# A GRU on one core: the last batches of a two-level fast product paired anew, and two pairs of PSUM seeds moved behind a projection

## The chip, the cores and the metric

The kernel runs on one core of a Trainium2 chip. The metric is the time of one execution on the device in microseconds (us). Three runs of the kernel before took 1289.52, 1290.0 and 1290.32 us, so the median is 1290.0 us. One further execution was taken with the hardware profiler on.

The engines are called PE (TensorE, matmuls; PEld is its weight load), DVE (VectorE), ACT (ScalarE), POOL (GpSimd) and SP (SyncE, which issues most transfers). PSUM is the memory that PE writes its sums to; a tile of PSUM here is one bank.

## What is computed

The reference is a gated recurrent layer with a residual: for 128 steps, on a batch of 64 rows of width 512, all in 32-bit floats.

```python
def step(h, inp):                       # 128 times
    x_t, prop = inp
    comb = concatenate([x_t, h])
    z = sigmoid(comb @ Wz + bz)
    r = sigmoid(comb @ Wr + br)
    h_cand = tanh(concatenate([x_t, r * h]) @ Wh + bh)
    h_new = (1.0 - z) * h + z * h_cand
    h_next = where(prop, tanh(h_new @ Wp + bp), h_new)   # prop: t % 4 == 3, not at t = 127
    return h_next, h_new
return x + ys                           # ys: the h_new of all steps
```

The part of each gate that comes from x doesn't depend on the recurrence. The part that comes from h does, and sets an order: R and Z need h, the candidate H needs r * h, the next step needs h_new. In every fourth step the projection P follows.

## The kernel before, in words

**Recurrent part.** The batch of 64 is cut into two halves of 32 rows, half 0 and half 1, which run through the same steps with an offset. `half(h)` (L781) is a generator that writes the instructions of one half; the loop at L882 alternates between the two by columns of matmul issued, with half 1 starting 700 columns behind. A gate of one half is four products (L218); each product is two matmuls (L207 to L216), and the profile shows a product as four records on line L209. The gates R, Z, H and, at a projection step, P are written in this order.

Each half has its own PSUM tile, rec_0 or rec_1, whose first part takes R and whose second part takes H and P. Z of both halves has a third tile, rec_z. Before a gate's products run, ACT copies the part that comes from x into the gate's place (`seed`, L376, copy on L379); the products add to it. The seed of R for step t+1 is normally written right after R of step t has been read (L801), the seed of H after tanh of H has been read (L854), the seed of Z after half 1's h (L856). Two steps are exceptions. R's seeds for step 4 are written in step 3, after Z's sigmoid of half 1 (L818 to L820). R's seeds for step 124 are written in step 123, after the Z seed of half 1 (L857 to L859), which is ahead of the projection's products. At a projection step, the bias of P is copied into H's place (L852) and the seed of H for the next step follows the tanh of P (L871).

After a gate, ACT applies the sigmoid or tanh (L235), DVE multiplies and subtracts (L798, L812, L840, L849) and transposes (L238) for the next gate.

**Part from x.** It is computed in groups of four steps (g is the group, LAST = 31 the one of steps 124 to 127), by a two-level scheme that saves products. A group needs up to seven outer products, numbered 1 to 7 (8 to 11 are forms used at both ends). `batch(n, ms)` (L454) takes one or two of them and makes seven kinds of inner unit, in the order 2, 7, 1, 5, 4, 6, 3. A batch has as many units of each kind as it has outer products (product 10 counts twice, for it has two terms), each of 192 columns. The sums lie in the scratch banks a, x or y (alternating between batches), q and r. They are evicted by ACT and DVE at the ends of kinds:

- after kind 7, ACT copies x to cx (L485);
- after kind 1, ACT copies q to cq (L485);
- after kind 5, DVE adds r to cx and a to cq (L502, L503);
- after kind 6, ACT copies q again and DVE adds it (L508);
- after kind 3, DVE adds r and x to the last copy (L511, L512).

Units of a later kind or batch that write the same bank wait for these. R's sigmoid also writes into a free part of the bank r. POOL then combines outer products into the tiles cp that the seeds read (L544, L549; 128 x 768 elements). A cp tile holds two steps. In the last group, steps 126 and 127 are computed plainly (`plain`, units of 256 columns, a DVE add on L417 per gate), and steps 124 and 125 by `pair_left` and `pair_right` (L583, L587), two POOL operations each.

**Order.** All units form one queue (`put`, L391). Each step takes units from it at three places: between the gates Z and H, after H, and, at a projection step, after P. How many is written down per step: `PLACES` for the eight steps that repeat, `HEAD` for steps 0 to 4, `TAIL` for steps 118 to 127 (T is 128). The queue is filled by `begin` (L649), and for the last group at step 118 (T - 10). `behind_step` (L704) issues the POOL operations behind each step, in the end the sum of x and h (L756), and the transfers of the output on SP (L766).

The engines run their instructions in the order written, each when its operands are ready.

Of the kernel before, what the change touches and what calls it, by code (L numbers as in the profile page):

```python
# [18 lines left out]
def kernel(  # L19
# [15 lines left out]
    B, T, D = x.shape  # L35
    H = h0.shape[1]
    P = 128
    S = 2
# [8 lines left out]
    LAST = T // Q4 - 1  # L47
    R, Z, H_ = range(3)
# [115 lines left out]
    def gate_ps(i, h):  # L164
        return rec[2][:, 0] if i == Z else rec[h][:, 0 if i == R else 1]
# [210 lines left out]
    def seed(i, t, h):  # L376
        if t < T:
            rows = slice(None) if i == Z else ts(h, 2 * V)
            nc.scalar.copy(  # L379
                gate_ps(i, h)[rows].rearrange("p d (c n) -> p d c n", c=C),  # L380
                G[t][rows, :, :, i, :].rearrange("p c d n -> p d c n"),
            )
# [8 lines left out]
    def put(units):  # L391
        for unit, cols, bank, end, read in units:
            queue.append((unit, cols, reader.get(bank, -1), end))
            for b in read:
                reader[b] = len(queue) - 1
# [38 lines left out]
    def plain(t, gates=(R, Z, H_)):  # L434
        order = [(e, k) for e in gates for k in range(K)]
        if t == Q4 - 1:
            order = [(e, k) for k in range(K) for e in gates]
        return [
            plain_unit(
                t, e, k, k == 0, *((lambda: add_bias(t, gates), gates) if (e, k) == order[-1] else ())  # L440
            )
            for e, k in order
        ]
# [88 lines left out]
    def batches(g):  # L532
        if g * Q4 >= T:
            return []
        ms = [(g, i) for i in (1, 2, 6, 5, 7, 3, 4)]
        if g + 1 < LAST:
            ms += [(g + 1, i) for i in (1, 6, 2, 5, 3, 7, 4)]
        return sum((batch((g, n), ms[2 * n : 2 * n + 2]) for n in range(7) if 2 * n < len(ms)), [])

    def flat(v):  # L540
# [17 lines left out]
    def outer_1(g):  # L558
        with_bias(g, 1, bias0)
# [17 lines left out]
    def outer_c22(g):  # L577
        add(c_block(g, 1, 1), m_(g, 7), m_(g, 5))

    def outer_c21(g):  # L580
        add(c_block(g, 1, 0), m_(g, 7), m_(g, 4))

    def pair_left(a, p1, p2, g=1):  # L583
        with_bias(g, p2, bias0)
        add(c_block(g, a, 0), m_(g, p1), m_(g, p2))

    def pair_right(a, p1, x_, g=1):  # L587
        with_bias(g, x_, bias_x[:, 1])
        add(c_block(g, a, 1), m_(g, p1), m_(g, x_))
# [4 lines left out]
    )  # L594
    HEAD = {0: (12, 12, 0), 1: (8, 6, 0), 2: (16, 12, 0), 3: (8, 6, 8), 4: (6, 8, 0)}
    TAIL = {
        T - 10: (1, 7, 0), T - 9: (3, 7, 5), T - 8: (1, 7, 0), T - 7: (1, 6, 0), T - 6: (0, 6, 0),
        T - 5: (0, 4, 3), T - 4: (0, 5, 0), T - 3: (0, 5, 0), T - 2: (0, 5, 0), T - 1: (0, 0, 0),
    }

    idle(40)
# [47 lines left out]
    def begin(t):  # L649
        u = (t - 3) % 8  # L650
        even = FIRST + 2 * ((t - 3) // 8)
        if t == 0:
            put(plain(2) + plain(3))
        elif t == 1:
            put(batch((1, 0), [(1, 1), (1, 2)]))
        elif t == 2:
            put(batch((1, 1), [(1, 10), (1, 11)]) + batch((1, 2), [(1, 8), (1, 9)]))
        elif t == 3:
            put(batches(FIRST))
        elif u == 7:  # L660
            put(batches(even + 2))
        if t == T - 10:
            put(
                batch((LAST, 0), [(LAST, 1), (LAST, 2)])
                + batch((LAST, 1), [(LAST, 10)])
                + plain(T - 1, (R,))[:2]
                + plain(T - 2)
                + plain(T - 1, (R,))[2:]
                + plain(T - 1, (H_,))
                + plain(T - 1, (Z,))  # L670
            )
# [32 lines left out]
    def behind_step(t, duo, u, h_new):  # L704
        g, j = divmod(t, Q4)
        even, odd = FIRST + 2 * duo, FIRST + 2 * duo + 1
        if t == T - 8:
            pair_left(0, 1, 2, LAST)
        elif t == T - 6:
            pair_right(0, 1, 10, LAST)  # L710
        if t == 3:
            pair_left(1, 8, 9)
            pair_right(1, 8, 11)

        if duo >= 0:
            if u == 0 and duo >= 1 and odd - 2 < LAST:
                outer_c22(odd - 2)
                outer_c21(odd - 2)
            if even * Q4 < T:
                if u == 0:  # L720
                    sum_s34(even)
                elif u == 1:
                    outer_1(even)
                    outer_c11(even)
                    sum_raw12(odd)
                elif u == 2:
                    outer_u1(even)
                    outer_5(even)
                    sum_raw4(even)
                elif u == 3:  # L730
                    outer_c12(even)
                    outer_u2(even)
                    outer_c22(even)
                    if odd < LAST:
                        sum_s12(odd)
                elif u == 4:
                    if odd < LAST:
                        sum_s34(odd)
                    outer_c21(even)
                    if odd < LAST:  # L740
                        outer_1(odd)
                elif u == 5 and odd < LAST:
                    sum_raw4(odd)
                elif u == 6 and odd < LAST:
                    outer_u1(odd)
                    outer_c11(odd)
                elif u == 7 and odd < LAST:
                    outer_5(odd)
                    outer_c12(odd)
        if duo >= -1 and (even + 2) * Q4 < T:  # L750
            if t == 2 or (u == 6 and duo >= 0):
                sum_raw12(even + 2)
            if u == 7:
                sum_s12(even + 2)
        if t < T - 1:
            nc.gpsimd.tensor_add(xr[g][:, j], xr[g][:, j], h_new)  # L756

        n = 0
        if t >= T - CHUNK:
            n = 3 if t == T - 2 else 0  # L760
        elif j == Q4 - 1:
            n = 4
        if n:
            for h in range(S):
                for q in range(NQ):
                    nc.sync.dma_start(  # L766
                        out=out[ts(h, V), t - n + 1 : t + 1, ts(q, J)],
                        in_=xr[g][part(q), j - n + 1 : j + 1, h, :],
                    )
        if j == 1 and g >= 1 and (g + 1) * Q4 < T:  # L770
            new_xr(g + 1)
            load_x(xr[g + 1], (g + 1) * Q4, Q4)
        if t in (1, 2):
            load_xs(t + 2)
        if duo >= 0:
            if u == 3:
                load_xs(odd + 2)
            elif u == 6:
                load_xs(even + 4)

    def half(h):  # L781

        for t in range(T):
# [5 lines left out]
            if h == 0:  # L789
                begin(t)  # L790
# [18 lines left out]
            if h == 1:  # L809
                for i in range(S):  # L810
                    crossed(z[:, i, :], i, Z, AF.Sigmoid)
                nc.vector.scalar_tensor_tensor(  # L812
                    out=keep, in0=z, scalar=1.0, in1=h_old, op0=ALU.subtract, op1=ALU.mult
                )
                join(t, duo, u, 1)
                if t == 1:
                    sum_raw34(1)
                if t == 3:  # L818
                    for i in range(S):
                        seed(R, t + 1, i)  # L820
                if last:
                    nc.gpsimd.tensor_sub(xr[g][:, j], xr[g][:, j], keep)
                if t == 0:
                    sum_outer()
                    join_x(1, 0)
                    join_x(1, 1)
                    sum_raw12(1)
                    sum_inner(6, nc.gpsimd)
                    sum_inner_1(6, nc.gpsimd)
                if t == 2:  # L830
                    for n in range(2, 4):
                        join_x(2, n)
# [21 lines left out]
                seed(H_, t + 1, h)  # L854
            if h == 1 and t != T - 2:
                seed(Z, t + 1, 0)  # L856
            if h == 1 and t == T - 5:  # L857
                for i in range(S):
                    seed(R, t + 1, i)  # L859
            state[t + 1] = h_new, hT  # L860
            yield from fill(places[1], h)
            if h == 1 and t == T - 2:
# [1 line left out]
            if prop:  # L864
                yield from gate(P_, h, hT, wp)
                h_next = new_two("hprop", t)
                hT = new_turned("hT", "hpT", t)
                crossed(h_next[:, h, :], h, P_, AF.Tanh)
                turn(hT[:, h, :], h_next[:, h, :])
                if t < T - 2:  # L870
                    seed(H_, t + 1, h)  # L871
                state[t + 1] = h_next, hT
                yield from fill(places[2], h)
            if h == 1:
# [7 lines left out]
    while any(live):  # L882
        h = 0 if live[0] and (not live[1] or at[0] <= at[1]) else 1
# [46 lines left out]
```

## Time and profile before

| | us |
|---|---|
| median of three runs | 1290.0 |
| the profiled execution | 1288.07 |
| its span | 1286.2 |
| busy time of PE within it | 1253.8 |
| busy time of POOL | 886.1 |
| busy time of ACT | 835.5 |
| busy time of DVE | 781.3 |
| transfers, mean | 47 GB/s |

The span runs from the first to the last instruction that the profile shows. The rest of the profiled execution's time, 1.87 us, lies around it. A row of the timeline gives the start in us from the beginning of the span, the duration, the engine, the line, the operation, what it writes and reads, the size, and how many instructions of this form follow each other. In brackets stands the idle time of the engine ahead of it, and what ended that idle time. A busy PE isn't PE at its peak, because matmuls overlap: several records are in flight at a time, and the duration of one is longer than the time to the next.

### The profile page before, as it was taken

To read this page: it belongs to the slowest core of one execution; us is meant where nothing else is said; L and a number is where in the kernel's file an instruction comes from. 1 tells how busy PE (TensorE), PEld (TensorE's weight loads), DVE (VectorE), ACT (ScalarE), POOL (GpSimd) and SP (SyncE) were. 2 spreads that over 40 slices of the span, in tenths; PEclk is the share of its full clock that TensorE was granted. 3 is DMA by queue.
4 is the path that set the end of the run, shared out by engine and by line. 5 is a ranking of instruction groups with operands and counts; after the bars stand their busy time and mean duration, and the time that the engine had idled before them with its cause. 6 is when DMAs were issued, how large, how long until landed. Compare 5 with 4: busy or idle time off the path is not lost.

```text
span 1286.2 us, 60724 instructions
## 1 busy us (share of the span) xinstructions
PE 1253.8 (97%) x25968; PEld 1167.4 (91%) x25968; DVE 781.3 (61%) x2166; ACT 835.5 (65%) x2688; POOL 886.1 (69%) x1027
## 2 busy tenths in 40 slices
PE   6989999999999999999999999999999999999988
PEld 2679999999999999999999999999999999999766
DVE  4646666656665666666666666666656666666544
ACT  1446666666666666666766667666676666666655
POOL 5449777777677776777787677776777787677430
PEclk9989999999999999999999999999999999999999
DMA  8302211111121111111111121111112112111100
GB/s 224 82 19 52 52 36 41 47 36 52 40 61 39 29 45 51 52 36 53 38 34 52 46 58 36 33 45 45 52 36 57 38 28 52 52 35 36 26 25 21
DMA packets 113365, 60.82 MB, mean 47 GB/s; under 512 B 12969, under 2 KB 109481, under 8 KB 113097
## 3 DMA queue, kind: packets, MB, share of 16 engines
q1 hardware_dynamic: 110628, 53.46, 16.1%
q8 instruction: 205, 3.36, 1.1%
q10 hardware_dynamic: 2212, 3.34, 1.0%
q14 instruction: 64, 0.52, 0.1%
q0 software_dynamic: 256, 0.14, 0.1%
HBM read 40.11 MB, written 16.78 MB: 44 GB/s over the span
## 4 chain that ended last, share of the span: by engine, by line
PE 93%; DMA 2%; POOL 1%; issue 1%; ACT 1%; DVE 1%; SPq 0%; ACTq 0%; POOLq 0%; DVEq 0%
PE rec L209 42%; PE rec_z L209 15%; PE scratch_r L209 13%; PE scratch_q L209 10%; PE scratch_a L209 5%; PE scratch_x L209 4%; PE scratch_y L209 4%; DMA wx<-in_L_cond_Wh_dram 1%; DMA wh<-in_L_cond_Wh_dram 1%; DMA wh<-in_L_cond_Wr_dram 0%; POOL cp L544 0%; DMA wx<-in_L_cond_Wr_dram 0%; ACT rec_z L235 0%; POOL mb L549 0%; DVE rec_z L840 0%
## 5 line engine op out<-in xcount | busy, mean ns | idle before, releaser
L209 PE MATMUL rec<-wh,rhT 128*32 128x256 f32 x4096 | 377.1, 381 | 4.5 <-ACT rec L379 4.5
L209 PE MATMUL rec<-wh,hT 128*32 128x256 f32 x3072 | 281.3, 379 | 0.3 <-DVE hT L238 0.3
L209 PE MATMUL rec_z<-wh,hT 128*32 128x256 f32 x3072 | 281.3, 379 | 0.1
L209 PEld LDWEIGHTS rec<-wh,rhT 128*32 128x32 f32 x4096 | 251.2, 110 | 23.6 <-ACT rec L379 4.9
L379 ACT COPY rec<-cp 64x256 f32<-64x256 f32 x512 | 189.8, 371 | 42.6 <-DVE cp L417 17.0
L235 ACT ACTIVATE scratch_r<-rec 64x128 f32<-64x128 f32 x512 | 128.0, 250 | 134.0 <-PE rec L209 70.7
L209 PEld LDWEIGHTS rec_z<-wh,hT 128*32 128x32 f32 x3072 | 193.3, 110 | 7.1 <-ACT rec_z L379 0.6
L209 PEld LDWEIGHTS rec<-wh,hT 128*32 128x32 f32 x3072 | 187.2, 110 | 12.9 <-ACT c L235 1.5
L235 ACT ACTIVATE rec_z<-rec_z 64x128 f32<-64x128 f32 x512 | 128.0, 250 | 96.1 <-PE rec_z L209 84.0
L235 ACT ACTIVATE c<-rec 64x128 f32<-64x128 f32 x512 | 138.9, 271 | 64.2 <-PE rec L209 52.9
L756 POOL TENSOR_TENSOR xr<-xr,h 128x256 f32<-128x256 f32 x127 | 93.0, 732 | 88.0 <-DVE h L849 79.8
L544 POOL TENSOR_TENSOR mb<-mb,mb 128x768 f32<-128x768 f32 x58 | 106.2, 1831 | 67.1 <-DVE mb L512 67.0
L544 POOL TENSOR_TENSOR cp<-mb,mb 128x768 f32<-128x768 f32 x75 | 137.1, 1828 | 7.3 <-DVE mb L512 3.7
L544 POOL TENSOR_TENSOR cp<-mb 128x768 f32<-128x768 f32 x47 | 86.1, 1832 | 56.9 <-ACT rec_z L379 55.4
L812 DVE SCALAR_TENSOR_TENSOR keep<-rec_z,h 128x256 f32<-128x256 f32 x96 | 40.7, 424 | 133.8 <-ACT rec_z L235 128.6
L209 PE MATMUL scratch_r<-tw,s 128*32 128x192 f32 x928 | 120.9, 326 | 0.0
L485 ACT COPY cq<-scratch_q 128x384 f32<-128x384 f32 (+1 forms) x214 | 102.4, 478 | 19.5 <-PE scratch_q L209 18.0
L502 DVE TENSOR_TENSOR cx<-scratch_r,cx 128x384 f32<-128x384 f32 (+1 forms) x107 | 59.2, 554 | 86.5 <-PE scratch_r L209 76.6
L549 POOL TENSOR_TENSOR mb<-mb,bias_x 128x768 f32<-128x768 f32 x35 | 64.0, 1829 | 58.2 <-DVE mb L512 58.2
L209 PE MATMUL scratch_q<-tt,s 128*32 128x192 f32 x928 | 103.7, 326 | 0.0
L508 DVE TENSOR_TENSOR mb<-scratch_q,cx 128x384 f32<-128x384 f32 (+1 forms) x107 | 59.2, 553 | 58.5 <-ACT cq L485 58.4
L798 DVE TENSOR_TENSOR rh<-scratch_r,h 128x128 f32<-128x128 f32 x192 | 56.0, 291 | 63.3 <-ACT scratch_r L235 63.3
(182 smaller groups left out, 3844.6 us busy)
## 6 DMA issues: line engine op xcount, KB each, us to landing
out_dram<-xr SPq DMA_DIRECT2D x249, 64.0 KB, 1.8
xr<-in_x_dram SPq DMA_DIRECT2D x248, 64.0 KB, 2.2
xs<-in_x_dram SPq DMA_DIRECT2D x240, 64.0 KB, 2.2
wp<-in_L_cond_Wp_dram SPq DMA_DIRECT2D x4, 256.0 KB, 5.6
wx<-in_L_cond_Wr_dram SPq DMA_DIRECT2D x4, 128.0 KB, 2.7
wx<-in_L_cond_Wr_dram ACTq DMA_DIRECT2D x4, 128.0 KB, 2.8
wx<-in_L_cond_Wz_dram SPq DMA_DIRECT2D x2, 256.0 KB, 6.6
wx<-in_L_cond_Wz_dram ACTq DMA_DIRECT2D x2, 256.0 KB, 6.7
```

What stands on the lines that cost most here:

```text
L209: nc.tensor.matmul(ps[part(2 * h + c)], lhsT=left, rhs=rhs(c), start=start, stop=True, skip_group_check=True,)
L235: nc.scalar.activation(dst[ts(d, 2 * V)], gate_ps(i, h)[ts(h, 2 * V), d, :], func)
L379: nc.scalar.copy(gate_ps(i, h)[rows].rearrange("p d (c n) -> p d c n", c=C), G[t][rows, :, :, i, :].rearrange("p c d n -> p d c n"),)
L485: nc.scalar.copy(c[:, :nm], ps[:, :nm])
L502: nc.vector.tensor_add(T2[what][:, :nm], r_ps[:, :nm], T2[what][:, :nm])
L508: nc.vector.tensor_add(blocks(1, 1), runs(q_ps[:, :nm]), runs(T2[what][:, :nm]))
L544: nc.gpsimd.tensor_add(dst, a, b)
L549: nc.gpsimd.tensor_add(m, m, v.unsqueeze(1).to_broadcast([P, 2, 3 * J]))
L756: nc.gpsimd.tensor_add(xr[g][:, j], xr[g][:, j], h_new)
L798: nc.vector.tensor_mul(rh[:, h, :], r_, h_old[:, h, :])
L812: nc.vector.scalar_tensor_tensor(out=keep, in0=z, scalar=1.0, in1=h_old, op0=ALU.subtract, op1=ALU.mult)
```

## The change

There are four edits.

1. `batches(30)` no longer takes the outer product (30, 4), which was alone in its batch. At step 118 the queue gets the batch of (30, 4) and (31, 1), fourteen units, and the batch of (31, 2) and (31, 10), twenty-one units. Before, the queue had a batch of (30, 4) with seven units, a batch of (31, 1) and (31, 2) with fourteen, and a batch of (31, 10) with fourteen.
2. `TAIL` places them anew: step 118 takes 14 units (5 and 9) in place of 8, step 119 takes 13 in place of 15, steps 121 and 122 take 6 and 5 in place of 7 and 6, and 125 and 126 are set to 4 in place of 5.
3. `pair_left` and `pair_right` are both issued behind step 121. Before they stood behind step 120 and step 122.
4. In steps 3 and 123, the R seeds for the next step are written behind the tanh of the projection of each half, in front of the H seed. The H seed loses a condition that held at every projection step.

```diff
@@ batches
         ms = [(g, i) for i in (1, 2, 6, 5, 7, 3, 4)]
         if g + 1 < LAST:
             ms += [(g + 1, i) for i in (1, 6, 2, 5, 3, 7, 4)]
+        else:
+            ms.pop()
@@
     TAIL = {
-        T - 10: (1, 7, 0), T - 9: (3, 7, 5), T - 8: (1, 7, 0), T - 7: (1, 6, 0), T - 6: (0, 6, 0),
-        T - 5: (0, 4, 3), T - 4: (0, 5, 0), T - 3: (0, 5, 0), T - 2: (0, 5, 0), T - 1: (0, 0, 0),
+        T - 10: (5, 9, 0), T - 9: (1, 7, 5), T - 8: (1, 7, 0), T - 7: (1, 5, 0), T - 6: (0, 5, 0),
+        T - 5: (0, 4, 3), T - 4: (0, 5, 0), T - 3: (0, 4, 0), T - 2: (0, 4, 0), T - 1: (0, 0, 0),
     }
@@ begin
         if t == T - 10:
             put(
-                batch((LAST, 0), [(LAST, 1), (LAST, 2)])
-                + batch((LAST, 1), [(LAST, 10)])
+                batch((LAST, 0), [(LAST - 1, 4), (LAST, 1)])
+                + batch((LAST, 1), [(LAST, 2), (LAST, 10)])
                 + plain(T - 1, (R,))[:2]
                 ...
@@ behind_step
-        if t == T - 8:
+        if t == T - 7:
             pair_left(0, 1, 2, LAST)
-        elif t == T - 6:
             pair_right(0, 1, 10, LAST)
@@ half, behind Z
-                if t == 3:
-                    for i in range(S):
-                        seed(R, t + 1, i)
@@ half, behind H
-            if h == 1 and t == T - 5:
-                for i in range(S):
-                    seed(R, t + 1, i)
@@ half, behind the projection
                 crossed(h_next[:, h, :], h, P_, AF.Tanh)
                 turn(hT[:, h, :], h_next[:, h, :])
-                if t < T - 2:
-                    seed(H_, t + 1, h)
+                if t in (3, T - 5):
+                    seed(R, t + 1, h)
+                seed(H_, t + 1, h)
```

## The prediction

> **What bounds the kernel now.** I read the page's summary and its forty slices first, then the chain that ended last.
>
> ```profile
> span 1286.2 us, 60724 instructions
> PE 1253.8 (97%) x25968; PEld 1167.4 (91%) x25968; DVE 781.3 (61%) x2166; ACT 835.5 (65%) x2688; POOL 886.1 (69%) x1027
> PE   6989999999999999999999999999999999999988
> PEclk9989999999999999999999999999999999999999
> PE 93%; DMA 2%; POOL 1%; issue 1%; ACT 1%; DVE 1%; SPq 0%; ACTq 0%; POOLq 0%; DVEq 0%
> ```
>
> TensorE is the chain. The slices are below 9 only at the start, in the third slice (64 to 96 us, the one place where the clock row dips too) and in the last two. The view by stretches of time puts numbers on that.
>
> ```profile
> 600.00:676.88 76.88, 76.88 (x1623) 73.62 (x1616) 48.37 (x135) 52.63 (x169) 56.63 (x67) 1.00 0.17 44
> 79.20:81.40 2.20, 0.00 (x0) 0.00 (x0) 0.00 (x0) 0.00 (x0) 2.13 (x2) 1.00 0.01 4
> 83.67:88.24 4.57, 4.57 (x50) 3.58 (x54) 1.28 (x3) 2.09 (x6) 0.00 (x0) 0.50 0.02 4
> 1195.50:1257.30 61.80, 53.72 (x1051) 43.29 (x1045) 28.62 (x89) 37.05 (x124) 18.83 (x15) 1.00 0.11 28
> ```
>
> The columns are stretch, length, busy time of PE, PEld, DVE, ACT, POOL, granted clock, DMA share, GB/s. Eight steps in the middle (first row) have no idle TensorE at all, so nothing done off TensorE counts there, and the change doesn't touch them. What can move is the hole around step 3 (second and third rows) and the 61.80 − 53.72 = 8.08 us idle in steps 118 to 123 (fourth row). TensorE's own work is the same before and after: units are paired and reordered, none is added or dropped. In the middle row a product of one half (four records) takes about 0.216 us at 256 columns and 0.16 us at 192: 832 records at 0.054 are 44.9 us and the other 784 at 0.0405 give the rest.
>
> **Seeds for step 4.** The timeline around step 3:
>
> ```profile
> 76.75 0.31 DVE L238 STREAM_TRANSPOSE rhT<-rh 128x128 f32<-128x128 f32 x1
> 81.41 1.80 POOL L544 TENSOR_TENSOR cp<-mb,mb 128x768 f32<-128x768 f32 x1
> 83.25 0.77 ACT L379 COPY rec<-cp 64x256 f32<-64x256 f32 x2 [4.55 <-POOL cp L544]
> 83.67 0.64 PE L209 MATMUL rec<-wh,rhT 128*32 128x256 f32 x2 [4.50 <-ACT rec L379]
> 90.12 0.38 ACT L379 COPY rec_z<-cp 128x256 f32<-128x256 f32 x1 [0.28 <-DVE h L849]
> 91.55 0.55 ACT L235 ACTIVATE hprop<-rec 64x128 f32<-64x128 f32 x2 [0.55 <-PE rec L209]
> 92.13 0.37 ACT L379 COPY rec<-cp 64x256 f32<-64x256 f32 x1
> 93.93 0.38 PE L209 MATMUL rec<-wh,hpT 128*32 128x256 f32 x2
> ```
>
> The H gate of step 3 had rhT at 77.06 but went at 83.67, because the R seeds of step 4 were written ahead of it into its own PSUM tile, and they wait for the POOL sum in cp (ready 83.21). TensorE stands 4.50 us. The clock is half from 81.40 to 88.24, and the 4.57 us of work in it would be 2.28 at full rate: 2.28 lost. Sum 6.78. An idle break costs about 0.3 more than its row shows, since the last matmul's busy time runs 0.3 past the slot it is issued in; I put the whole hole at 7.0.
>
> Seeds moved: H of step 3 then waits for rhT alone. What is late next is the Z seed of step 4, which reads the same cp. Moved forward by 7.0 it would be due at 90.12 − 7.0 = 83.1, and cp is there at 83.21: up to 0.1 on ACT, which the copies behind it have room for (ACT is free 0.55 us ahead of the projection's tanh). The two moved copies are 2 × 0.37 on ACT between the two projection tanhs and behind them. The second tanh comes 0.4 later. The R gate of step 4 starts 2.4 us after the first tanh (93.93 against 91.55), and its seed lies right behind that tanh where the H seed now is (92.13), so it is covered; if it weren't, 0.4 to 0.8. I take a gain of 6.9, bounds 6.0 and 7.1.
>
> **Waits that go in the tail.** These are the breaks of TensorE in the fourth stretch, with what each stands behind.
>
> ```profile
> 1200.23 1.82 POOL L544 TENSOR_TENSOR cp<-cp,mb 128x768 f32<-128x768 f32 x1 [4.67 <-DVE mb L512]
> 1202.08 0.37 ACT L379 COPY rec<-cp 64x256 f32<-64x256 f32 x1 [1.78 <-POOL cp L544]
> 1203.39 0.36 PE L209 MATMUL scratch_r<-tw,s4r 128*32 128x192 f32 x2 [1.71 <-DVE rh L798]
> 1209.60 0.36 PE L209 MATMUL scratch_q<-wx,xT 128*32 128x192 f32 x2 [1.50 <-DVE mb L508]
> 1229.84 0.36 PE L209 MATMUL scratch_q<-tt,s12r 128*32 128x192 f32 x2 [1.45 <-ACT cq L485]
> 1239.34 0.41 PE L209 MATMUL scratch_q<-wx,xT 128*32 128x256 f32 x2 [1.83 <-DVE mb L508]
> 1248.47 0.41 PE L209 MATMUL rec<-wp,hT 128*32 128x256 f32 x2 [1.59 <-ACT rec L379]
> 1248.05 0.76 ACT L379 COPY rec<-cp 64x256 f32<-64x256 f32 x2
> ```
>
> The five bracketed idles sum to 8.08, the whole idle of the stretch; with 0.3 each the loss is 9.6. 1203: R of step 119 scratch bank r waits for a sigmoid queued behind a seed for step 120 that waits for cp, which waits for L512; in the new order the batch that feeds it ends 7 units earlier, so cp is in time. 1209, 1229 and 1239: a bank is used again after a batch of one product, whose kinds of unit are one unit long, so the evicting engine has half the time; with two products per batch there are two units per half between. 1248: the P gate of step 123 waits for the two R seeds of step 124, ahead of it in its tile; they move behind it. I take all five as gone: 9.5.
>
> **Waits that come in the tail.** First, step 118 now runs a whole batch further (fourteen units in two places), and its unit of kind 5 needs bank r, freed by the add at L511 of the batch before. Step 117 shows the same order one step earlier.
>
> ```profile
> 1187.02 0.55 DVE L511 TENSOR_TENSOR mb<-scratch_r,cq 128x384 f32<-128x384 f32 x1
> 1188.31 0.56 ACT L235 ACTIVATE c<-rec 64x128 f32<-64x128 f32 x2
> 1189.01 0.36 PE L209 MATMUL scratch_r<-tw,s 128*32 128x192 f32 x2
> 1189.56 0.31 DVE L238 STREAM_TRANSPOSE hT<-h 128x128 f32<-128x128 f32 x1
> ```
>
> There L511 came 2 us ahead of its reader. In the built order of step 118 it stands on DVE behind both halves' transposes of h, so in these times it ends about 1189.56 + 0.31 + 0.55 − 0.2 = 1190.2 (0.2 for the one unit fewer ahead of H in 118), against a reader due at 1189.01: 1.2 us. It could be 0 (fewer units placed in front) or 1.6; 1.2 is by the nearest row. Behind the waiting matmul stand all of TensorE's later units, and who waits for these is the R gate of 119.
>
> Second, steps short of cover. From the last Z record of half 1 to the next R (or P) of half 0 a chain runs through ACT and DVE that no engine shortens; step 126 shows it bare.
>
> ```profile
> 1270.89 1.11 PE L209 MATMUL rec<-wh,rhT 128*32 128x256 f32 x16
> 1271.17 1.09 ACT L235 ACTIVATE rec_z<-rec_z 64x128 f32<-64x128 f32 x4 [0.75 <-PE rec_z L209]
> 1272.29 1.16 ACT L235 ACTIVATE c<-rec 64x128 f32<-64x128 f32 x4
> 1273.27 0.29 DVE L849 TENSOR_TENSOR h<-rec_z,keep 128x128 f32<-128x128 f32 x1
> 1273.60 0.31 DVE L238 STREAM_TRANSPOSE hT<-h 128x128 f32<-128x128 f32 x1
> 1274.06 0.41 PE L209 MATMUL rec<-wh,hT 128*32 128x256 f32 x2 [0.33 <-DVE hT L238]
> ```
>
> 1274.06 − 1270.89 = 3.17 us (Z's sigmoids, tanh of half 0, two multiplies, a transpose). Under it lie the products that TensorE issues in between, counted in the new order:
> - 119 and 120: 7 of 256 columns and 12 of 192, 1.51 + 1.95 = 3.46: no loss.
> - 121: 7 and 8, 2.81: 0.36.
> - 122: 14 of 256, 3.02: 0.14, and 0.3 where H waits for R's sigmoid behind L511.
> - 123, to the P gate: 12, 2.59: 0.57.
> - 124's R gates behind the moved seeds: tanh, R seed and H seed follow each other, 0.47 (by two copies of 0.37 of which 0.27 is covered); 0 to 0.8.
> - 125 and 126 lose a unit each that steps 118 to 123 now carry: two products of 0.216 each, 0.44 + 0.43, though both steps stay as long as the chain makes them.
> New: 1.2 + 0.36 + 0.44 + 0.57 + 0.47 + 0.87 = 3.9. Tail: 9.5 − 3.9 = 5.6 gained.
>
> **Other edits, at nothing.**
>
> ```profile
> L756 POOL TENSOR_TENSOR xr<-xr,h 128x256 f32<-128x256 f32 x127 | 93.0, 732 | 88.0 <-DVE h L849 79.8
> L549 POOL TENSOR_TENSOR mb<-mb,bias_x 128x768 f32<-128x768 f32 x35 | 64.0, 1829 | 58.2 <-DVE mb L512 58.2
> 1264.80:1272.30 7.50, 7.50 (x144) 6.26 (x140) 4.11 (x13) 4.95 (x18) 0.73 (x1) 1.00 0.01 2
> ```
>
> Five DVE evictions and three ACT copies fewer: ACT is idle for 40% of the fourth stretch and DVE for more, so these were not the bound. POOL's count is the same; the four adds of the last pairs (4 × 1.83 = 7.3 us) now run in one piece behind step 121, in front of that step's xr add. DVE's h of step 123 waits for that add, since h has two buffers. The pairs' last batch ends in the first units of step 122, about 6.4 us after 121's Z; 7.3 and 0.73 more end the add at 14.5. That h comes two steps of about 7.5 (third row) and the chain's 3.2 after 121's Z, at 18.2: 3.7 us hide it. SP's output transfers queue behind the xr add of step 123, not of 121: nothing waits for them until the end. The dropped condition on the H seed changes no instruction.
>
> **Sum.** 6.9 + 5.6 = 12.5. The profiled execution took 1288.07 us (span 1286.2 and 1.87 around it), 1.93 under the median of 1290.0; 1288.07 − 12.5 = 1275.6, and with 1.93 again 1277.5.
>
> **The clock, as rule and row.** In the head the idle begins at 83.67 − 4.50 = 79.17, the clock halves 2.2 us into it and is full again 6.84 us later; tail breaks up to 1.83 us leave it at 1.00. [...]
>
> **Rivals.**
> - *Head only* (0.13). New waits at 118 and in 121 to 125 take back what the tail frees, since latency, not order, sets its steps. For: its last steps are already chain-bound. Against: the five breaks each have a named cause that the new order removes. 1290.0 − 6.9 = 1283.1.
> - *Tail only* (0.06). The head's wait goes over to the Z seed, which reads the same cp. Against: due at 83.1, there at 83.21. 1290.0 − 5.6 = 1284.4.
> - *Better* (0.05). The 118 wait isn't there: 1277.5 − 1.2 = 1276.3.
> [...]
> - *No effect* (0.03): other waits stand right behind each removed one, 1290. The rows show no second waiter in the head, where rhT was 6.6 us early.
>
> **Chances.** Forecast 0.68, head only 0.13, tail only 0.06, better 0.05, slower 0.05, no effect 0.03. A measurement of this kernel can tell about 0.2% (2.6 us) from no change. Faster 0.68 + 0.13 + 0.06 + 0.05 = 0.92; same 0.03; slower 0.05. The range runs from 1274.5 (no wait at 118, head 7.1, half of the small tail losses covered) to 1284.5 (tail only). It leaves out 0.08 by cases and a little beside them; the likeliest case's own range is 1275.5 to 1280.
>
> **What would show it.** Right: the 4.50 us before H of step 3 are gone, with the clock at 1.00 throughout steps 3 and 4; no break over 1.5 us in 118 to 123; a wait of about 1.2 for L511 in 118; P of 123 after 0.6. Wrong: a clock under 1.00 at 80 to 90 us, a POOL wait before DVE's h of step 123, or breaks near 2 us in 119 to 124.

## The result

| | before | after |
|---|---|---|
| median, us | 1289.76 (4 runs) | 1276.51 (4 runs, 1275.99 to 1277.99) |
| ratio, 95% interval | | 0.9899 (0.9887 to 0.9912) |
| profiled execution, us | 1288.07 | 1276.41 |
| its span, us | 1286.2 | 1274.6 |

The kernel after is 13.2 us faster; 1277.5 was forecast. The page of the kernel after, its first part and two rows of its slices:

```profile
span 1274.6 us, 60714 instructions
PE 1253.5 (98%) x25968; PEld 1164.3 (91%) x25968; DVE 781.5 (61%) x2161; ACT 835.6 (66%) x2685; POOL 886.8 (70%) x1027
PE   6999999999999999999999999999999999999997
PEclk8999999999999999999999999999999999999999
```

TensorE has as many matmuls as before. The third slice and the last but one are full now. Its busy time over the whole span is nearly the same (1253.5 us against 1253.8), but only because two differences cancel: while the weights come in, up to the end of the first step's Z gate, TensorE was busy 27.08 us at a granted clock of 0.83, against 25.28 us at 0.91 before, and in the head, as the rows further down show, it was busy 2.46 us less.

To put the time in its place I use one instruction that every step has, DVE's `keep` behind Z's sigmoids. The head is the stretch between the `keep`s of steps 3 and 5. Two groups of rows of the timeline, first of the kernel before, at steps 3, 5, 118 and 127:

```profile
78.73 0.42 DVE L812 SCALAR_TENSOR_TENSOR keep<-rec_z,h 128x256 f32<-128x256 f32 x1 [1.67 <-ACT rec_z L235]
109.47 0.42 DVE L812 SCALAR_TENSOR_TENSOR keep<-rec_z,h 128x256 f32<-128x256 f32 x1 [1.65 <-ACT rec_z L235]
1195.49 0.42 DVE L812 SCALAR_TENSOR_TENSOR keep<-rec_z,h 128x256 f32<-128x256 f32 x1 [1.32 <-ACT rec_z L235]
1280.12 0.42 DVE L812 SCALAR_TENSOR_TENSOR keep<-rec_z,h 128x256 f32<-128x256 f32 x1 [1.65 <-ACT rec_z L235]
```

and of the kernel after, at the same steps:

```profile
79.60 0.42 DVE L813 SCALAR_TENSOR_TENSOR keep<-rec_z,h 128x256 f32<-128x256 f32 x1 [1.66 <-ACT rec_z L235]
103.39 0.42 DVE L813 SCALAR_TENSOR_TENSOR keep<-rec_z,h 128x256 f32<-128x256 f32 x1 [1.65 <-ACT rec_z L235]
1189.47 0.42 DVE L813 SCALAR_TENSOR_TENSOR keep<-rec_z,h 128x256 f32<-128x256 f32 x1 [1.32 <-ACT rec_z L235]
1268.59 0.42 DVE L813 SCALAR_TENSOR_TENSOR keep<-rec_z,h 128x256 f32<-128x256 f32 x1 [1.65 <-ACT rec_z L235]
```

From step 3 to step 5: 30.74 us before, 23.79 after, 6.95 less. From 5 to 118: 1086.02 and 1086.08. From 118 to 127, which is called the tail from here on: 84.63 and 79.12, 5.51 less. Together 12.46; the forecast had 6.9 and 5.6. The stretch up to step 3, where the weights come in, was 0.87 longer in this one execution, so the two profiles differ by 11.7 and not by 12.5.

The head of the kernel after, rows of its timeline:

```profile
79.84 0.38 PE L209 MATMUL rec<-wh,rhT 128*32 128x256 f32 x1
82.35 1.83 POOL L546 TENSOR_TENSOR cp<-mb,mb 128x768 f32<-128x768 f32 x1
84.21 0.38 ACT L379 COPY rec_z<-cp 128x256 f32<-128x256 f32 x1 [0.45 <-POOL cp L546]
85.47 0.55 ACT L235 ACTIVATE hprop<-rec 64x128 f32<-64x128 f32 x2 [0.38 <-PE rec L209]
86.06 0.77 ACT L379 COPY rec<-cp 64x256 f32<-64x256 f32 x2
87.85 0.40 PE L209 MATMUL rec<-wh,hpT 128*32 128x256 f32 x2
```

H of step 3 goes at 79.84 with no idle time in front, while cp is still being made. The first reader of cp is now the Z seed at 84.21, 0.03 us behind the end of POOL's add; ACT stood 0.45 us for it. The moved R seed of half 0 and the H seed behind it (the two copies in a row at 86.06) are done at 86.83, 1.0 us ahead of R of step 4. The head and the tail from `keep` to `keep`, in the view of stretches, first before, then after:

```profile
78.73:109.47 30.74, 26.25 (x518) 22.92 (x514) 14.56 (x41) 16.20 (x50) 20.80 (x20) 0.89 0.07 17
1195.49:1280.12 84.63, 76.08 (x1446) 60.45 (x1438) 40.84 (x128) 51.15 (x174) 21.04 (x18) 1.00 0.10 25
```

```profile
79.60:103.39 23.79, 23.79 (x518) 21.83 (x514) 14.55 (x40) 16.12 (x50) 20.73 (x20) 1.00 0.08 19
1189.47:1268.59 79.12, 76.37 (x1440) 60.77 (x1434) 40.43 (x123) 50.81 (x171) 21.09 (x18) 1.00 0.11 27
```

In the head, the idle time of TensorE went from 30.74 − 26.25 = 4.49 us to none, and the same 518 records take 2.46 us less, with the clock at 1.00 in place of 0.89: the 6.95 is both together. In the tail TensorE idles 79.12 − 76.37 = 2.75 us where it idled 8.55. The waits that are left there, and what they stand behind (waits first, then timeline):

```profile
PE rec L209 <- DVE hT L238: 1.7, 4, 0.8
PE scratch_r L209 <- DVE mb L511: 0.8, 1, 0.8
```

```profile
1193.18 0.52 DVE L511 TENSOR_TENSOR mb<-scratch_r,cq 128x384 f32<-128x384 f32 x1
1193.75 0.36 PE L209 MATMUL scratch_r<-tw,s4r 128*32 128x192 f32 x2 [0.79 <-DVE mb L511]
1223.37 0.53 ACT L235 ACTIVATE scratch_r<-rec 64x128 f32<-64x128 f32 x2 [1.15 <-DVE mb L511]
1229.49 1.83 POOL L546 TENSOR_TENSOR cp<-mb,mb 128x768 f32<-128x768 f32 x1
1231.27 1.42 POOL L757 TENSOR_TENSOR xr<-xr,h 128x256 f32<-128x256 f32 x2
```

None of the five old breaks is among them. Four are waits for the transpose of h, that is, for the chain of 3.17 us; one is the forecast wait for L511 in step 118.

### The profile page after: what moved, and what is told of

Read it like the earlier page. It is cut to its first block, busy times and chain, and to the rows that moved or that the text cites. A ratio compares the mean times of both kernels' runs of the same rounds, so it can differ in the third digit from the quotient of the medians.

```text
span 1274.6 us, 60714 instructions
## 1 busy us (share of the span) xinstructions
PE 1253.5 (98%) x25968; PEld 1164.3 (91%) x25968; DVE 781.5 (61%) x2161; ACT 835.6 (66%) x2685; POOL 886.8 (70%) x1027
## 4 chain that ended last, share of the span: by engine, by line
PE 95%; DMA 2%; ACT 1%; issue 1%; DVE 1%; SPq 0%; ACTq 0%; POOLq 0%; POOL 0%; DVEq 0%
PE rec L209 44%; PE rec_z L209 16%; PE scratch_r L209 13%; PE scratch_q L209 10%; PE scratch_a L209 5%; PE scratch_y L209 4%; PE scratch_x L209 4%; DMA wx<-in_L_cond_Wh_dram 1%; DMA wh<-in_L_cond_Wh_dram 1%; SPq L94 0%; DMA wx<-in_L_cond_Wr_dram 0%; DMA wh<-in_L_cond_Wr_dram 0%; ACT rec_z L235 0%; ACT c L235 0%; DMA xr<-in_x_dram 0%
## 5 line engine op out<-in xcount | busy, mean ns | idle before, releaser
L485 ACT COPY cq<-scratch_q 128x384 f32<-128x384 f32 x212 | 102.1, 482 | 19.8 <-PE scratch_q L209 18.3
L502 DVE TENSOR_TENSOR cx<-scratch_r,cx 128x384 f32<-128x384 f32 x106 | 59.1, 558 | 80.6 <-PE scratch_r L209 69.3
L508 DVE TENSOR_TENSOR mb<-scratch_q,cx 128x384 f32<-128x384 f32 x106 | 59.1, 557 | 57.9 <-ACT cq L485 57.7
L209 PE MATMUL rec<-wh,hpT 128*32 128x256 f32 x992 | 91.4, 379 | 0.1
```

The lines of the kernel that those rows point to most:

```text
L209: nc.tensor.matmul(ps[part(2 * h + c)], lhsT=left, rhs=rhs(c), start=start, stop=True, skip_group_check=True,)
L485: nc.scalar.copy(c[:, :nm], ps[:, :nm])
L502: nc.vector.tensor_add(T2[what][:, :nm], r_ps[:, :nm], T2[what][:, :nm])
L508: nc.vector.tensor_add(blocks(1, 1), runs(q_ps[:, :nm]), runs(T2[what][:, :nm]))
```

## Experiments

Each run was timed against the kernel before in five rounds on the same chip. Not all runs had the same chip; the medians of the kernel before in the three groups of runs were 1289.37, 1289.52 and 1289.69 us. "Tail" is the stretch between the `keep` of steps 118 and 127 in its trace, "head" the one between those of steps 3 and 5. Each is from one profile; the loading of the weights at the start varies by more than 1 us between runs (last section), so where an edit is worth less than that, the stretch tells it better than the median.

**Seeds alone.** The kernel before, with the old lines of both seeds taken out and this put in behind the projection:

```diff
+                if t in (3, T - 5):
+                    seed(R, t + 1, h)
+                seed(H_, t + 1, h)
```

> The kernel before with nothing changed but the R seeds of steps 4 and 124, both behind the projection. Theory (each removed wait is worth what its own row shows): 6.9 us in the head; at step 123 the 1.9 us in front of the P gate becomes at most 0.6 and 0.5 us comes at the R gate of step 124, so 0.8 us there. 1289.8 - 7.7 = 1282.1. Rival (the head's hole only moves, and the tail makes the gain): 1287 to 1289.

1281.27 us, ratio 0.9937 (0.9925 to 0.995). Head 23.79, tail 84.14: 6.95 and 0.49 less than before. The head gave what was expected; the tail gave less than the 0.8 expected.

**Seeds of step 4 alone.** The same with `if t == 3`, and the old place kept for step 124.

> The kernel before with only the R seeds of step 4 moved; those of step 124 stay where they were. Theory: 6.9 us less than before, 1282.9, with the clock at 1.00 throughout steps 3 and 4; the 1.6 us idle in front of the P gate of step 123 stays. Rival (the seeds at step 124 make most of the gain): less than 2 us.

1282.67 us, ratio 0.9945 (0.9931 to 0.9958). Head 23.80, tail 84.64. The head's gain is whole by itself, and the hole doesn't go elsewhere.

**Pairing and places alone.** The kernel after, with the R seeds of steps 4 and 124 written where the kernel before has them.

> The kernel after with the R seeds of steps 4 and 124 in their old places. Theory: the head's hole of 4.5 us and its half clock stand, the P gate of step 123 waits about 1.6 us for the seeds again; the rest of the tail is as after. 5.6 - 0.8 = 4.8 us less than before, 1285.0. Rival (the new order only shifts the tail's idle time into later steps, and the seeds make all of the gain): within 2 us of before, 1288 to 1290.

1284.14 us, ratio 0.9959 (0.9946 to 0.9971). The hole is there again:

```profile
84.67 0.64 PE L209 MATMUL rec<-wh,rhT 128*32 128x256 f32 x2 [4.49 <-ACT rec L379]
```

Tail 79.63, 5.0 less than before. The gains against before of this run and of the seeds alone, 5.2 and 8.1 us, add up to 13.3, which is all of the change. So the rivals *head only* and *tail only* have fallen.

**New places with the old pairing.**

```diff
-        else:
-            ms.pop()
...
-                batch((LAST, 0), [(LAST - 1, 4), (LAST, 1)])
-                + batch((LAST, 1), [(LAST, 2), (LAST, 10)])
+                batch((LAST, 0), [(LAST, 1), (LAST, 2)])
+                + batch((LAST, 1), [(LAST, 10)])
```

> The kernel after with the batches of the kernel before: (30,4) alone, (31,1) with (31,2), (31,10) alone; the places of the units, the pairs behind step 121 and the seeds are as after, and the number of units is the same. Theory (a batch of one product reuses its banks before they are evicted): breaks of 1.4 to 1.8 us with L508 or L485 behind them are back, two or three of them, 3.5 to 6 us slower than after: 1280 to 1282.5. Rival (the number of units per step makes the gain and the pairing is worth nothing): 1276 to 1277.5.

1280.58 us, ratio 0.993 (0.9918 to 0.9943), tail 82.44. From its timeline and its waits:

```profile
1194.48 0.36 PE L209 MATMUL scratch_r<-tw,s4r 128*32 128x192 f32 x2 [1.44 <-DVE mb L511]
```

```profile
PE scratch_y L209 <- ACT cx L485: 1.3, 1, 1.3
```

Breaks came back, and by the medians their size was as expected, 4.1 us; by the tail it is 3.3, just under the range. But they stand behind L511 (1.44 in place of 0.79) and the copy of cx, not behind L508 and the copy of cq. The first is in the batch of (30, 4), which alone in its batch reaches kind 5 after three units in place of six. The second is not in a short batch at all: ACT copies cx of the batch of (31, 1) and (31, 2) at 1205.66, behind both tanhs of step 119. So the reason given fits the first at most.

**Old places with the new pairing.** The kernel after with the `TAIL` of before, and the pairs behind step 122, where their batch then ends.

> The kernel after with the table of places of the kernel before; the new pairing and the moved seeds stay, and the pairs stand behind step 122, where their batch then ends. Theory (the pairing alone isn't the gain: the places decide whether the batch that feeds cp for step 120 ends early in step 118): the wait of 1.7 us in front of R's reader in step 119 is back, and a wait for L485 as in the run with units later, 1.6; the wait for L511 in step 118 goes (1.1), and 125 and 126 have their units again (0.9): 1276.5 + 2.0 + 1.9 - 2.0 = 1278.4. Rival (the pairing makes the gain and the places nothing): 1276 to 1277.

1279.39 us, ratio 0.9917 (0.9904 to 0.9931), tail 80.58. Timeline:

```profile
1197.78 0.41 PE L209 MATMUL rec<-wh,rhT 128*32 128x256 f32 x2 [0.39 <-ACT rec L379]
1203.36 0.36 PE L209 MATMUL scratch_q<-tt,s4r 128*32 128x192 f32 x2 [1.68 <-ACT cq L485]
```

The wait for the copy of cq came as expected; the one for cp of step 120 came with 0.39 in front of H, and not 1.7, though ACT waited 1.77 for that cp. With the other in place, the new places are worth 1.5 us of the tail and the new pairing 3.3 (80.58 and 82.44 against 79.12). Neither makes the gain alone.

**Step 118 at 6 and 8.**

```diff
-        T - 10: (5, 9, 0)
+        T - 10: (6, 8, 0)
```

> The kernel after with one unit of step 118 moved from behind H to in front of it (6 and 8 in place of 5 and 9), so that the batch before ends ahead of H, as in step 117. Theory (the wait of 0.79 us for L511 in step 118 comes from L511 standing on DVE behind the transposes of both halves): the wait is gone, 0.8 to 1.1 us faster than after, 1275.5. Rival (bank r is too short of time whatever the order on DVE): the same wait, 1276.5.

1275.45 us, ratio 0.9893 (0.9878 to 0.9907), tail 78.09, 1.03 less than after. Of the two waits of TensorE one is left:

```profile
PE rec L209 <- DVE hT L238: 1.6, 4, 0.8
```

It was the place of L511 in DVE's order, then, and not the bank. The stretch of the trace shows it; the medians of the two kernels lie 1.1 apart, and their intervals overlap.

**Units moved to the steps that the chain bounds.**

```diff
-        T - 10: (5, 9, 0), ... T - 7: (1, 5, 0), T - 6: (0, 5, 0),
-        T - 5: (0, 4, 3),
+        T - 10: (6, 4, 0), ... T - 7: (1, 6, 0), T - 6: (0, 6, 0),
+        T - 5: (0, 5, 3),
...
-        if t == T - 7:
+        if t == T - 6:
             pair_left(0, 1, 2, LAST)
```

> The kernel after with step 118 at 6 and 4 units, and one unit more in each of steps 121, 122, 123 (behind H) and 126; the pairs stand behind step 122, since their batch now ends there. Theory (steps 121 to 126 are as long as the chain through ACT and DVE, so a unit costs nothing in them, and 0.33 to 0.43 us in a step that TensorE bounds): the wait in 118 is gone too; 0.9 + 4 x 0.35 = 2.3 us faster than after, 1274.2. Rival (the pairs' POOL block now ends too late for the R seeds of step 124 or for DVE's h of step 124): a wait of 2 to 4 us in step 123 or 124, 1277 to 1279.

1278.14 us, ratio 0.9912 (0.9897 to 0.9927), tail 80.28. Slower by 1.2 in the tail, and for neither reason given. Timeline:

```profile
1192.05 0.41 PE L209 MATMUL rec<-wh,hT 128*32 128x256 f32 x2 [0.53 <-DVE hT L238]
1200.98 0.36 PE L209 MATMUL scratch_q<-tt,s4r 128*32 128x192 f32 x2 [1.60 <-ACT cq L485]
```

With five units fewer behind H than in the kernel after, step 118 itself was short of cover (0.53). And all later units shifted against the steps, so that the two products of kind 1 fell on both sides of H in step 119; their copy to cq then stood on ACT behind the tanhs. Units can't be counted alone: a shift of the queue moves every kind against the gates.

**R seeds of step 124 in the usual place.**

```diff
-            if t not in (3, T - 5):
+            if t != 3:
...
-                if t in (3, T - 5):
+                if t == 3:
                     seed(R, t + 1, h)
```

> The kernel after with the R seeds of step 124 in the usual place, right behind the R sigmoid of step 123; those of step 4 stay behind the projection. Theory (with the pairs done by 1231.3, the seeds need not wait there, and the 0.4 to 0.5 us in front of step 124's R gates come from the two copies behind each tanh): 0.2 to 0.5 us faster than after, 1276.2. Rival (the P gate of step 123 waits for the seeds in its tile as before): 1 to 2 us slower than after, 1277.5 to 1278.5.

1276.49 us, ratio 0.9897 (0.988 to 0.9913): the median is that of the kernel after. In the trace the tail is 78.33, 0.79 less. That profile came to step 0 1.55 us later than the one of the kernel after, so the two don't contradict each other, but by its median alone this run is inconclusive. The run below with three edits mended has this one among them.

**cp late by one add, and by two.** The kernel after with this behind `pair_right` at step 3, for n = 1 and 2; the add repeats the last one and gives the same values.

```diff
             pair_right(0, 1, 10)
+            for _ in range(n):
+                add(c_block(1, 0, 1), m_(1, 1), m_(1, 10))
```

> The kernel after with the last POOL add that makes cp for steps 4 and 5 done twice, so that cp is there 1.83 us later; nothing else changes. Theory (the Z seed of step 4 has only about 0.1 us to spare and stands on ACT in front of a copy and the projection's tanh; behind them TensorE has about 1 us of cover): 0.4 to 1.5 us slower than after, clock at 1.00: 1277.0 to 1278.0. Rival (there was more slack in the head than the rows show, and the gain didn't hang on cp being just in time): no change, 1276.5. Second rival (the clock halves at any wait in the head): 3 us or more, 1279.5.

1279.11 us, ratio 0.9919 (0.9904 to 0.9934). Head 24.89, 1.10 longer than after, with the clock at 1.00. Timeline:

```profile
87.51 0.38 ACT L379 COPY rec_z<-cp 128x256 f32<-128x256 f32 x1 [2.33 <-POOL cp L546]
118.20 0.36 PE L209 MATMUL scratch_x<-tt,s4r 128*32 128x192 f32 x2 [0.43 <-POOL s4r L312]
```

The Z seed waited on ACT as it should. Another 0.7 us was lost in step 6 (second row): POOL, 1.83 us behind, came late with a sum for the batches there. That I had not thought of. Of the 2.6 us by the medians, 0.8 is left, which is within what the loading varies. By its median the run lies above the range expected and near the second rival's time; that rival falls by the clock of 1.00 and by the head.

> The kernel after with the last POOL add that makes cp for steps 4 and 5 done three times, so that cp is there 3.66 us later. One extra add cost 1.1 us between steps 3 and 5. Theory of a fixed cover: the second costs its full 1.83 us, 2.9 together, and if the idle time of TensorE passes what keeps the clock (between 1.83 and 2.24 us by the kernel before) up to 2.3 us of half clock on top: 1279.4 to 1281.7 with the clock under 1.00 in step 4. Rival (a wait of under 3 us never halves the clock): 1279.4 with the clock at 1.00.

1280.79 us, ratio 0.9931 (0.9919 to 0.9944). Head 28.33, 4.54 longer than after. The break, and the clock in three stretches of 3.41 us around it:

```profile
89.91 0.54 PE L209 MATMUL scratch_q<-wx,xT 128*32 128x192 f32 x2 [2.75 <-DVE mb L508]
```

```profile
86.25:89.66 3.41, 0.91 (x22) 0.50 (x14) 0.37 (x1) 1.24 (x4) 2.02 (x2) 1.00 0.00 0
89.66:93.07 3.41, 3.16 (x40) 2.05 (x44) 1.65 (x5) 2.56 (x8) 2.13 (x2) 0.51 0.02 5
93.07:96.48 3.41, 3.41 (x72) 3.22 (x68) 1.81 (x5) 2.03 (x7) 3.33 (x3) 0.99 0.00 0
```

2.75 idle, some 0.3 beside it, and 3.16 us of work at half rate (1.58): 4.6. So with a wait of 2.75 us the clock was granted at 0.51 over the 3.41 us from 89.66 on, and the rival has fallen.

**Three edits mended.** The kernel after with step 118 at (6, 8, 0), step 119 at (1, 7, 4), step 121 at (1, 6, 0), and the R seeds of step 124 in the usual place.

> The kernel after with three edits: step 118 at 6 and 8 units; the R seeds of step 124 in the usual place; one unit of step 119 (behind the projection) moved on to step 121 (behind H). Theory: 1.0 + 0.8 by the traces of the first two alone, and 0.3 to 0.4 for the unit: 2.2 us faster than after, 1274.3. Rival (the same chain sets the end whichever wait is taken away): 1275.5 or more.

1274.46 us (1273.85 to 1275.05), ratio 0.9881 (0.9868 to 0.9895); tail 77.00, 2.12 less than after, as the sum said. It is the fastest of all, 2.05 us below the kernel after by the medians, though the two intervals against before still touch. What waits there:

```profile
PE rec L209 <- DVE hT L238: 1.4, 3, 0.8
```

**TensorE kept busy in the hole.** The kernel before with this in front of H's products.

```diff
+            if t == 3 and h == 0:
+                for i in range(76):
+                    nc.tensor.matmul(
+                        scratch[4][part(i % NQ), 3 * J :],
+                        lhsT=wx[:, 0, R, :V],
+                        rhs=wx[:, 1, R, :J],
+                        start=False,
+                        stop=True,
+                        skip_group_check=True,
+                    )
             yield from gate(H_, h, rhT, wh[H_])
```

> The kernel before with 76 matmuls of 128 columns added in front of the H gate of step 3, half 0; they write to a part of a scratch bank that nothing reads, and fill the hole of 4.5 us. Their results are not used. Theory (of the 6.9 us that the moved seeds of step 4 save, 2.3 are the half clock that follows from the idle time): with TensorE kept busy the clock stays at 1.00 and the kernel is 2 to 2.5 us faster than before, 1287.3, though it has more work. Rival (the hole's whole price is its idle time, and the clock would be back by itself): no faster than before, 1289.5 to 1290.

1286.97 us, ratio 0.9978 (0.997 to 0.9987). Groups, then timeline, then stretches:

```profile
L837 PE MATMUL scratch_y<-wx 128*32 128x128 f32 x152 | 4.3, 273 | 0.0
```

```profile
85.37 0.41 PE L209 MATMUL rec<-wh,rhT 128*32 128x256 f32 x2 [0.39 <-ACT rec L379]
```

```profile
80.40:85.37 4.97, 4.58 (x164) 4.28 (x157) 0.41 (x1) 0.40 (x2) 4.44 (x4) 1.00 0.02 5
85.37:90.00 4.63, 4.63 (x101) 3.87 (x103) 2.77 (x8) 3.41 (x10) 0.00 (x0) 1.00 0.01 4
```

H still waits for the seeds, but the clock is 1.00 and the head 28.62 in place of 30.74. More work made the kernel faster by 2.7 us; the head alone tells 2.12, against 2.28 for the half clock in the forecast's sum. The other 4.83 are the hole.

## Why the prediction was right

By its own steps, with "lost" as the length of a step between two `keep`s less its matmuls at the steady rate. A product (0.216 us) that lies at a `keep` can be counted on either side, so neighbouring rows are uncertain by that much:

| | before | forecast for after | after |
|---|---|---|---|
| steps 3 to 5 | 6.98 | 0.1 | 0.04 |
| step 118 | 2.04 | 1.2 | 1.09 |
| 119 and 120 | 2.02 | 0 | 0.00 |
| 121 and 122 | 3.64 | 0.36 + 0.44 | 0.80 |
| 123 | 1.90 | 0.57 + 0.47 | 1.17 |
| 124 | 0.13 | 0.13 | 0.35 |
| 125 | 0.13 | 0.57 | 0.57 |
| 126 | 1.23 | 1.66 | 1.66 |

- **The head.** 6.9 forecast, 6.95 in the trace. The two terms hold by themselves: the hole (4.8) and the half clock (2.28 forecast, 2.12 by keeping TensorE busy). "Up to 0.1 on ACT" for the Z seed was 0.17: ACT stood 0.45 in front of it, and DVE's h, which it also waits for, had been written 0.17 before cp was there. And one extra POOL add made it a wait of 2.33 on ACT. The seeds were covered; the margin was 1.0 us.
- **The five breaks of the tail.** All gone, as forecast (their 9.6 was carried on as 9.5). The reasons given were only partly shown. For the P gate's seeds, the run with seeds alone shows it, with a gain of 0.49. For the single-product batches, the run with the old pairing brought breaks back, but at other places than those named. For cp of step 120, the reason was wrong: cp isn't made earlier. Before, the POOL add for it ends 6.56 us after the `keep` of step 118 (1202.05); after, 6.60:

```profile
1194.24 1.83 POOL L546 TENSOR_TENSOR cp<-cp,mb 128x768 f32<-128x768 f32 x1 [4.68 <-DVE mb L512]
1196.37 0.53 ACT L235 ACTIVATE scratch_r<-rec 64x128 f32<-64x128 f32 x2 [0.78 <-PE rec L209]
```

  What moved is R's sigmoid of step 119, ahead of the seed that needs cp. It comes 6.90 us after that `keep` in place of 4.29, since step 118 has six more units to run. Before, it was this row of the timeline:

```profile
1199.78 0.53 ACT L235 ACTIVATE scratch_r<-rec 64x128 f32<-64x128 f32 x2
```

  The runs agree: with the new places and the old pairing nothing waits for this cp, and with the new pairing in the old places ACT waits 1.77 for it. So this term came out right by luck; the places gave it, not the pairing.
- **The wait for L511 in 118.** Its place and its cause were right (6 units in front of H remove it). 0.79 shown and 0.3 beside it, 1.09, against 1.2; without it the tail is 1.03 shorter.
- **Cover of 3.17 us.** The counts of products gave 121 to 126 to about 0.2 us each, which is as far as the rows can be trusted. The 1.15 us that R's sigmoid of step 122 waited for L511 cost what was forecast.
- **A term that was too small.** The R seeds of step 124 behind the projection were put at 0.47. Putting them back in the usual place saves 0.79, all of it between the `keep`s of steps 123 and 124 (10.55 us in place of 11.34). The bound of 0.8 held. That the pairs, moved to step 121, are done at 1231.3, when those seeds would be issued, so that this part of the change isn't needed any more, I hadn't seen.
- **The pairs' POOL block** cost nothing: the add to xr of step 121 behind it, the first of the two from 1231.27 on, ended about 1232.0, and DVE's h of step 123 wasn't written before 1235.44: 3.4 us of cover, against the 3.7 of the forecast. No run moved it alone.
- **The clock in the tail** stayed at 1.00 over the 79.12 us, where the longest wait of the two kinds that are left was 0.8 us; so the slower case, 0.05 among the chances, didn't happen. In the run with cp late by two adds, a break of 2.75 us came with a stretch of 3.41 us at 0.51, but in the head.
- **The total.** The medians differ by 13.2 us and the two stretches by 12.46. The rest, 0.8, is in neither and within what the loading of the weights varies; no run says where it comes from. It is most of the 1.0 us by which the forecast was high.

## What to carry to other kernels

When a PSUM tile is shared, look at who writes to it ahead of a gate: a copy that is only needed in the next step can hold this step's matmuls if it is written first, as it did here for 4.50 us. Price an idle TensorE by its clock too: here nearly a third of a hole's cost (2.12 of 6.95 us) came after it. And in a stretch that a fixed chain bounds, count the products issued under the chain; that count, and the place of each eviction in its engine's order, gave the time of ten steps to a few tenths.

## What the runs showed of the hardware

Where the clock was half, in the stretches looked at. From the kernel before, three that follow each other in the head; the last two are the 6.84 us of half clock:

```profile
77.98:81.40 3.42, 1.19 (x32) 0.72 (x21) 0.42 (x1) 0.65 (x3) 3.35 (x5) 1.00 0.01 2
81.40:84.82 3.42, 1.15 (x14) 0.96 (x18) 0.00 (x0) 1.23 (x4) 1.80 (x1) 0.50 0.00 0
84.82:88.24 3.42, 3.42 (x42) 2.62 (x37) 1.28 (x3) 1.27 (x4) 0.00 (x0) 0.50 0.03 5
```

In the first, TensorE was busy 35% of the time at 1.00, and the second was granted 0.50. In the second it was busy 34%, and the third was granted 0.50 too. In the third it was busy all the time, and the 3.41 us behind it were granted 1.00. In the run with two late adds, a stretch at 1.00 that was busy 27% stood ahead of one granted 0.51, and that one, busy 93%, ahead of one granted 0.99.

Two more stretches of that length come from the loading of the weights, first in the kernel after, then in the kernel before:

```profile
24.73:28.14 3.41, 1.28 (x24) 0.54 (x16) 3.27 (x4) 0.00 (x0) 3.33 (x4) 1.00 1.07 298
19.97:23.38 3.41, 1.46 (x28) 0.74 (x20) 3.32 (x3) 0.00 (x0) 3.37 (x3) 1.00 1.02 267
```

TensorE was busy 38% and 43% of them, and the 3.41 us behind each were granted 0.50 and 1.00. These are shares of the profile's records, whose ends are modelled. They tell what these stretches did; a rule for the clock was not shown.

The time until the `keep` of step 0, in which the weights are loaded, was between 39.06 and 41.49 us in fourteen profiles of kernels that are alike up to there. That spread of 2.4 us is more than each single edit of the places was worth, so the medians alone can't rank them. What makes it wasn't tried.
